# Last layer of a four-layer graph network: the pair product in two row halves of the array

## The chip, the cores and the metric

The kernel runs on one core of a Trainium2 chip. The metric is the device time of one execution in microseconds (us). A core has five engines with instruction queues of their own: PE (TensorE, matrix products; PEld is its loading of weights), DVE (VectorE), ACT (ScalarE), POOL (GpSimd) and SP (SyncE, which here only issues loads). Engines meet only through semaphores.

## The reference

Four graph layers over 4096 nodes with 64 features and a dense 4096x4096 f32 matrix `adj`, each followed by a residual sum and a layer norm. The change lies in the last layer, the hyperbolic one:

```python
def _mobius_add(x, y, c):
    x2 = sum(x * x); y2 = sum(y * y); xy = sum(x * y)
    num = (1.0 + 2.0 * c * xy + c * y2) * x + (1.0 - c * x2) * y
    den = 1.0 + 2.0 * c * xy + c ** 2 * x2 * y2
    return num / maximum(den, MIN_NORM)

sub = _mobius_add(-x_i, x_j, c);  sub_norm = norm(sub)
log_ij = 2.0 / (sqrt_c * lam_x) * arctanh(clip(sqrt_c * sub_norm)) * sub / sub_norm
agg = einsum('ij,ijc->ic', adj / deg, log_ij)
transformed = agg @ weight + bias
x = layernorm(x + expmap(0, transformed))
```

For every pair (i, j) a scalar function of the two points is needed, and then a weighted sum over j of vectors that are linear in x_j. The function depends on one number of the pair, v, which is a product of a vector of i and a vector of j.

## The kernel before, in words

The 4096 nodes are 32 blocks of 128, or 8 groups of 512 (`GB` = 4 blocks a group). Three layers run first; the last one is the block that opens with `with tc.tile_pool(name="o3"`, and its preparation is woven into the end of layer 2.

**Preparation.** `prepare(g)` computes, for the four blocks of a group, the squared norm `n2`, `inside` = 1 - n2, its sign `side`, two flags `sides` (inside or outside the ball), and `rabs` = 1/|inside|. It fills `nat_c` (the rows that the gather sums: x/|inside| in 63 columns, (1 + n2)/|inside| in the last) and `lx`, 66 columns: x, n2 and 1, each times 1/inside. `turn_prepared` transposes `lx` into 66 rows of `tr_a` and `sides` into 2 rows of `tr_o` (bf16, in the memory of `sp_two`), four 128x128 transposes each and one DVE copy each (`to_columns`, L214). `constants3` makes the constants: `to_right`, 66x66, that turns a left vector into a right one, `to_other`, 2x2, for the flags, and `wh_x`, the last weight padded with zeros below row 64.

**The loop.** A tile is a pair of groups (i, j) with j not before i in `seq`: 36 tiles, 8 of them diagonal. Each has two units n of two blocks, so there are NU = 72 units. `right(i)` makes the right operand of a row i: one f32 product of `to_right` with 512 columns of `tr_a`, copied by ACT to `rvs`, and one bf16 product of `to_other`, copied to `ros`. Then, for each unit:

- `product(n)`, L1359, PE: v for two blocks of j against 512 columns of i, two f32 matmuls that contract over 128 rows (66 of them carry data), each into a PSUM bank of its own. There are two `v_ps` buffers, so product(n + 2) waits for the last reader of v of unit n.
- `square(n)`, L1368, ACT: w = (1 + v)^2, the 1 by a bias column.
- `opposite(n)`, L1377, PE: two bf16 matmuls that add 2^60 to v where i and j lie on opposite sides.
- `less_one(n)`, L1385, DVE: w = max(w - 1, floor).
- Ln and Exp on ACT (L1550, L1551) give rt = sqrt(w); DVE adds v to it (L1575, the last reader of v); ACT takes Ln(1 + rt) (L1586) and Exp of w (L1577).
- two units later DVE forms f (L1560) and multiplies the tile of `adj` with it (`at_d`, L1563).
- `turn`, PE L1403: f is transposed, eight 128x128 transposes a unit, for the mirrored tile (j, i), and DVE multiplies (`at_m`, L1405, two a unit). A diagonal tile uses L1396 and L1398 instead.
- `gather`, PE L1419 and L1424: the sums over j for group i in the upper 64 columns of the array and those of the mirrored tile in the lower 64, issued in turns; DVE adds the mirrored sums to `tb` (L1435).

A list `seam` puts one step of other work behind each unit: the end of layer 2 for four groups (`ends`, whose last steps are `prepare` and `turn_prepared`), the `weights` and `factors` of the end, and `finals(g)` for each finished group (L1475 to the store of the output), which multiplies `tr_a` with `wh_x` (L1487).

What sets the order: each engine runs its queue in order. Operations marked `in_order` (the gather here) keep the order of the program among themselves; the rest is placed by the framework's scheduler from its estimates.

Of the kernel before, what the change touches and what calls it, by code (L numbers as in the profile page):

```python
# [9 lines left out]
F32 = mybir.dt.float32  # L10
# [50 lines left out]
def gnn4_kernel(  # L61
# [37 lines left out]
    def gcols(g):  # L99
        return slice(g * GW, (g + 1) * GW)  # L100
# [629 lines left out]

    nat_c = three.tile([P, NB, F], F32, name="nat_c")

    tr_o = sp_two.rearrange("p b f -> p (b f)")
    nat_b = three.tile([P, NB, F], F32, name="nat_b")
    middle = ctx.enter_context(ExitStack())
    late = middle.enter_context(tc.tile_pool(name="late", bufs=1))
# [361 lines left out]
    def prepare(g):  # L1098

        gs = gblocks(g)  # L1100
        xg = nat_a[:, gs, 0:F]
        sq = sm.tile([P, GB, F], F32, name="sq", tag="t0")
        nc.vector.tensor_tensor(sq, xg, xg, ALU.mult)
        nc.vector.tensor_reduce(n2[:, gs], sq, AX.X, ALU.add)
        nc.vector.tensor_scalar(inside[:, gs], n2[:, gs], -1.0, 1.0, ALU.mult, ALU.add)
        nc.vector.tensor_scalar(sides[:, gs, 0], inside[:, gs], 0.0, None, ALU.is_ge)
        nc.vector.tensor_scalar(sides[:, gs, 1], inside[:, gs], 0.0, None, ALU.is_lt)
        nc.vector.tensor_tensor(side[:, gs], sides[:, gs, 0], sides[:, gs, 1], ALU.subtract)
        nc.vector.tensor_tensor(rabs[:, gs], inside[:, gs], side[:, gs], ALU.mult)
        nc.vector.tensor_scalar_max(rabs[:, gs], rabs[:, gs], C_MIN)  # L1110
        nc.vector.reciprocal(rabs[:, gs], rabs[:, gs])
        lx = sm.tile([P, GB, F + 2], F32, name="lx")
        nc.vector.tensor_tensor(lx[:, :, F + 1], rabs[:, gs], side[:, gs], ALU.mult)
        nc.vector.tensor_tensor(lx[:, :, F], n2[:, gs], lx[:, :, F + 1], ALU.mult)
        nc.vector.tensor_tensor(lx[:, :, 0:F], xg, over_rows(lx[:, :, F + 1]), ALU.mult)
        nc.vector.tensor_tensor(nat_c[:, gs, 0 : F - 1], nat_a[:, gs, 0 : F - 1], over_rows(rabs[:, gs], F - 1), ALU.mult)
        nc.vector.scalar_tensor_tensor(nat_c[:, gs, F - 1], n2[:, gs], 1.0, rabs[:, gs], ALU.add, ALU.mult)
        left[g] = lx

    def turn_prepared(ps_p, g):  # L1120
        to_columns(ps_p, tr_a[0 : F + 2, gcols(g)], left.pop(g), F + 2, nc.vector.tensor_copy)
        to_columns(ps_p, tr_o[0:2, gcols(g)], sides[:, gblocks(g), :], 2, nc.vector.tensor_copy)

    def constants3():


        to_right = const.tile([P, F + 2], F32, name="to_right", tag="wih_pp")
        to_other = const.tile([P, 2], BF16, name="to_other", tag="wih_mm")

        spread = const.tile([P, F + 1], F32, name="spread", tag="whh_e")  # L1130
        wh_x = const.tile([P, F], F32, name="wh_x", tag="whh_n")
        nc.vector.memset(to_right, 0.0)
        nc.vector.tensor_scalar_mul(to_right[0:F, 0:F], ident[0:F, 0:F], -4.0)
        nc.vector.tensor_scalar_mul(to_right[F : F + 2, F : F + 1], ident[F : F + 2, F + 1 : F + 2], 2.0)
        nc.vector.tensor_scalar_mul(to_right[F : F + 2, F + 1 : F + 2], ident[F : F + 2, F : F + 1], 2.0)
        nc.vector.memset(to_other, 0.0)
        nc.vector.tensor_scalar_mul(to_other[0:2, 0:1], ident[0:2, 1:2], OPPOSITE)
        nc.vector.tensor_scalar_mul(to_other[0:2, 1:2], ident[0:2, 0:1], OPPOSITE)
        nc.vector.memset(wh_x, 0.0)
        nc.vector.tensor_copy(wh_x[0:F, :], wh)  # L1140
        nc.vector.tensor_copy(spread[:, 0 : F - 1], pair[:, 0 : F - 1])
        nc.vector.tensor_scalar(spread[:, F - 1 : F], pair[:, F - 1 : F], -1.0, None, ALU.add)
        nc.vector.tensor_copy(spread[:, F : F + 1], pair[:, F - 1 : F])
        return to_right, to_other, spread, wh_x
# [146 lines left out]

    with tc.tile_pool(name="o3", bufs=1) as op, tc.tile_pool(name="cols3", bufs=3) as cols_p, tc.tile_pool(
        name="w3", bufs=4
    ) as wp3, tc.tile_pool(name="el3", bufs=3) as el, tc.tile_pool(name="f3", bufs=2) as fp, tc.tile_pool(
# [9 lines left out]

        rvs = [op.tile([P, GW], F32, name=f"rv{q}") for q in range(2)]
        ros = [op.tile([P, GW], BF16, name=f"ro{q}") for q in range(2)]
        for t in rvs + ros:
            nc.gpsimd.memset(t, 0.0)  # L1310

        def right(i):
            q = seq.index(i) % 2
            ps = ps_p.tile([P, GW], F32, name="post", tag="post")
            nc.tensor.matmul(ps[0 : F + 2, :], lhsT=to_right, rhs=tr_a[:, gcols(i)], start=True, stop=True)
            nc.scalar.copy(rvs[q][0 : F + 2, :], ps[0 : F + 2, :])
            ps = ps_p.tile([P, GW], F32, name="post", tag="post")
            nc.tensor.matmul(ps[0:2, :], lhsT=to_other, rhs=tr_o[:, gcols(i)], start=True, stop=True)
            nc.scalar.copy(ros[q][0:2, :], ps[0:2, :])
# [30 lines left out]
        def product(n):  # L1350

            if n >= NU:
                return
            i, j = tiles[n // 2]
            vs[n] = ps_v.tile([P, HB, GW], F32, name="v_ps")
            cs = columns(n)
            for k in range(HB):
                jb = j * CB + (n % 2) * HB + k
                nc.tensor.matmul(  # L1359
                    vs[n][:, k, cs], lhsT=tr_a[:, cols(jb)], rhs=rights[i][0][:, cs], start=True, stop=True  # L1360
                )

        def square(n):
            if n >= NU:
                return
            ws[n] = wp3.tile([P, HB, GW], F32, name="w3")
            cs = columns(n)
            nc.scalar.activation(ws[n][:, :, cs], vs[n][:, :, cs], AF.Square, bias=one_col)  # L1368

        def opposite(n):  # L1370
            if n >= NU:
                return
            i, j = tiles[n // 2]
            cs = columns(n)
            for k in range(HB):
                jb = j * CB + (n % 2) * HB + k
                nc.tensor.matmul(  # L1377
                    vs[n][:, k, cs], lhsT=tr_o[:, cols(jb)], rhs=rights[i][1][:, cs], start=False, stop=True,
                    skip_group_check=True,
                )  # L1380
# [73 lines left out]
        def weights(ps_p):  # L1454
            ps = ps_p.tile([P, GW], F32, name="post", tag="post")
            nc.tensor.transpose(ps[0:F, 0:P], spread[:, 0:F], ident)
            t = sm.tile([F, P], F32, name="spread_t")
            nc.vector.tensor_copy(t, ps[0:F, 0:P])
            ps = ps_p.tile([P, GW], F32, name="post", tag="post")
            nc.tensor.matmul(ps[:, 0:F], lhsT=t, rhs=wh, start=True, stop=True)  # L1460
            nc.vector.tensor_copy(spread_w, ps[:, 0:F])


        def finals(g):
# [73 lines left out]
        while n < NU + 2 or turns or gathers:  # L1538
# [33 lines left out]
            for work in turned:  # L1572
                work()
            if n < NU:
                nc.vector.scalar_tensor_tensor(rt, vs[n][:, :, cs], V_FLOOR, rt, ALU.max, ALU.add)  # L1575
# [64 lines left out]
```

## Time and profile before

Three runs took 1536.35, 1538.62 and 1538.94 us. The profiled execution took 1536.75 us.

| | us |
|---|---|
| median of the runs | 1538.62 |
| profiled execution, whole | 1536.75 |
| its span, first to last instruction | 1535.0 |
| PE busy | 1408.3 (92%) |
| DVE busy | 1064.4 (69%) |
| ACT busy | 762.8 (50%) |
| POOL busy | 124.4 (8%) |
| last layer, first product to end | about 1062 to 1535 |
| its 72 units | 1062 to about 1510 |

The shares over the whole span mix four layers with different limits: in the first, PE and DVE are busy and the matrix is loaded at some 400 GB/s; in the last, DVE, PE and ACT are all near full and the loads are at 110 to 200 GB/s. An f32 matmul stands in the trace as two passes, so two matmuls of a product are four rows. "Idle before" is idle time of the engine in front of an instruction, with what ended it. Where two rows of PE start at the same time, two parts of the array work at once.

### The profile page before, as it was taken

To read this page: it belongs to the slowest core of one execution; us is meant where nothing else is said; L and a number is where in the kernel's file an instruction comes from. 1 tells how busy PE (TensorE), PEld (TensorE's weight loads), DVE (VectorE), ACT (ScalarE), POOL (GpSimd) and SP (SyncE) were. 2 spreads that over 40 slices of the span, in tenths; PEclk is the share of its full clock that TensorE was granted. 3 is DMA by queue.
4 is the path that set the end of the run, shared out by engine and by line. 5 is a ranking of instruction groups with operands and counts; after the bars stand their busy time and mean duration, and the time that the engine had idled before them with its cause. 6 is when DMAs were issued, how large, how long until landed. Compare 5 with 4: busy or idle time off the path is not lost.

```text
span 1535.0 us, 19444 instructions
## 1 busy us (share of the span) xinstructions
PE 1408.3 (92%) x7054; PEld 645.1 (42%) x7054; DVE 1064.4 (69%) x2121; ACT 762.8 (50%) x1267; POOL 124.4 (8%) x194
## 2 busy tenths in 40 slices
PE   5999999999999999889999999998888999899995
PEld 3555555554444333334443333333334434344343
DVE  5889989883000675657677322645999999899997
ACT  3554444432000111212222576655877999899995
POOL 3001100000000011222222200000000000000000
PEclk9999999999999999999999999999999999999997
DMA  9999999996787998878887655453134443445330
GB/s 291 411 406 409 413 409 399 385 357 265 247 278 270 373 387 322 278 280 316 301 317 286 193 170 176 155 165 156 65 141 155 170 168 138 167 160 191 150 114 11
DMA packets 103361, 385.40 MB, mean 251 GB/s; under 512 B 16340, under 2 KB 17368, under 8 KB 71256
## 3 DMA queue, kind: packets, MB, share of 16 engines
q1 hardware_dynamic: 84256, 296.78, 54.1%
q0 software_dynamic: 15616, 85.73, 13.7%
q10 hardware_dynamic: 3384, 1.56, 0.4%
q8 instruction: 58, 0.95, 0.2%
q14 instruction: 47, 0.39, 0.1%
HBM read 297.26 MB, written 85.20 MB: 249 GB/s over the span
## 4 chain that ended last, share of the span: by engine, by line
PE 65%; DVE 20%; ACT 7%; DMA 5%; issue 3%; SPq 0%; ACTq 0%; POOL 0%; DVEq 0%; POOLq 0%
PE tp L604 7%; PE pass L512 6%; PE w_ps L512 6%; PE v_ps L1359 5%; PE sums_ps L1419 4%; PE a_ps L1021 4%; PE cnt_ps L1242 4%; PE acc_ps L1198 4%; PE pass L505 4%; PE h_ps L505 4%; DVE at_m L1405 3%; DVE rt L1575 3%; PE p_ps L1004 2%; PE post L523 2%; ACT wt L1247 2%
## 5 line engine op out<-in xcount | busy, mean ns | idle before, releaser
L611 ACT COPY at<-tp 128x512 f32<-128x512 f32 x256 | 132.5, 599 | 134.6 <-issue 93.7
L1359 PE MATMUL v_ps<-rv,tr_a 128*128 128x512 f32 (+1 forms) x288 | 138.4, 604 | 33.6 <-DVE rt L1575 29.9
L1247 ACT ACTIVATE wt<-cnt_ps 128x512 uint16<-128x512 f32 x210 | 116.4, 594 | 73.8 <-PE cnt_ps L1242 69.6
L604 PE MATMUL tp<-ident,raw 128*128 128x128 f32 x1024 | 133.2, 284 | 14.5 <-DMA raw<-in_adj_dram 9.7
L637 DVE TENSOR_REDUCE dpart<-raw 128x4 f32<-128x2048 f32 x64 | 145.4, 2272 | 0.1
L639 DVE TENSOR_REDUCE lows<-raw 128x1 f32<-128x2048 f32 x64 | 145.4, 2272 | 0.0
L1419 PE MATMUL sums_ps<-at_d,nat_c 128*64 128x512 f32 x288 | 143.2, 619 | 1.4 <-DVE at_d L1563 1.0
L604 PEld LDWEIGHTS tp<-ident,raw 128*128 128x128 f32 x1024 | 116.5, 145 | 53.5 <-issue 30.7
L1021 PE MATMUL a_ps<-at,nat_a 128*64 128x512 f32 x512 | 126.3, 622 | 2.9 <-DVE at L987 2.9
L448 DVE TENSOR_SCALAR pos<-at 128x2048 fp8e4<-128x2048 f32 x72 | 87.6, 1232 | 49.3 <-DMA at<-adj_t 43.3
L1424 PE MATMUL sums_ps<-at_m,nat_c 128*64 128x512 f32 x224 | 111.0, 618 | 0.0
L512 PE MATMUL w_ps<-at,cheb_n 128*128 128x512 f32 x224 | 101.1, 595 | 0.0
L512 PE MATMUL pass<-at,cheb_n 128*128 128x512 f32 x224 | 98.3, 596 | 0.7 <-DVE cheb_n L665 0.7
L1586 ACT ACTIVATE rt<-rt,one_col 128x1024 f32<-128x1024 f32 x72 | 78.7, 1095 | 21.6 <-DVE rt L1575 21.4
L1359 PEld LDWEIGHTS v_ps<-rv,tr_a 128*128 128x128 f32 x288 | 51.9, 195 | 82.8 <-issue 43.4
L1242 PE MATMUL cnt_ps<-m,follow 128*64 128x512 fp8e4 x480 | 81.2, 391 | 5.1 <-ACT wt L1247 2.0
L1575 DVE SCALAR_TENSOR_TENSOR rt<-v_ps,rt 128x1024 f32<-128x1024 f32 x72 | 83.4, 1159 | 3.1 <-ACT rt L1551 2.9
L1560 DVE SCALAR_TENSOR_TENSOR f<-rt,w 128x1024 f32<-128x1024 f32 x72 | 83.0, 1160 | 1.3 <-ACT rt L1586 1.3
L1563 DVE TENSOR_TENSOR at_d<-at_d,f 128x1024 f32<-128x1024 f32 x72 | 83.4, 1159 | 0.1
L1405 DVE TENSOR_TENSOR at_m<-post,at_m 128x512 f32<-128x512 f32 x112 | 75.3, 685 | 10.1 <-PE post L1403 9.5
L1368 ACT ACTIVATE w<-v_ps,one_col 128x1024 f32<-128x1024 f32 x72 | 75.7, 1053 | 11.5 <-PE v_ps L1359 11.0
L1577 ACT ACTIVATE w<-w,half_shift 128x1024 f32<-128x1024 f32 x72 | 78.6, 1094 | 0.8
(368 smaller groups left out, 2269.7 us busy)
## 6 DMA issues: line engine op xcount, KB each, us to landing
at<-adj_t SPq DMA_DIRECT2D x122, 1024.0 KB, 6.6
raw<-in_adj_dram SPq DMA_DIRECT2D x64, 1024.0 KB, 12.3
adj_t<-at POOLq DMA_DIRECT2D x64, 1024.0 KB, 8.1
at_d<-adj_t SPq DMA_DIRECT2D x36, 1024.0 KB, 4.8
at_m<-adj_t SPq DMA_DIRECT2D x28, 1024.0 KB, 6.8
mask_t<-pos POOLq DMA_DIRECT2D x64, 256.0 KB, 6.2
m<-mask_t SPq DMA_DIRECT2D x120, 128.0 KB, 2.8
m<-mask_t SPq DMA_DIRECT2D x60, 256.0 KB, 4.0
```

The lines of the kernel that those rows point to most:

```text
L505: in_order(nc.tensor.matmul(ps[q * F : (q + 1) * F, :], lhsT=cheb_n[:, jb, k, :], rhs=rhs, start=first, stop=last, skip_group_check=True,))
L512: in_order(nc.tensor.matmul(ps, lhsT=cheb_n[:, jb, k : k + 2, :], rhs=rhs, start=first, stop=last))
L604: in_order(nc.tensor.transpose(tp[:, cols(b)], raw[:, b, cols(k)], ident))
L611: nc.scalar.copy(at[:, k, :], tp)
L637: in_order(nc.vector.tensor_reduce(dpart[:, g, c, :], raw, AX.X, ALU.add))
L639: in_order(nc.vector.tensor_reduce(lows[:, n : n + 1], raw.rearrange("p b j -> p (b j)"), AX.X, ALU.min))
L1021: in_order(nc.tensor.matmul(ps[q * F : (q + 1) * F, :], lhsT=nat_a[:, c * CB + k, 0:F], rhs=parts[q if signed else 0][:, k, :], start=(c = ...
L1242: in_order(nc.tensor.matmul(cnt[a][r * HP : (r + 1) * HP, :], lhsT=follow, rhs=chunks[c][odd][2 * a + r][:, k, :], start=(h == 2 * NB - 1) ...
L1247: in_order(nc.scalar.activation(wt[odd][a], cnt[a], AF.Relu, scale=-128.0))
L1359: nc.tensor.matmul(vs[n][:, k, cs], lhsT=tr_a[:, cols(jb)], rhs=rights[i][0][:, cs], start=True, stop=True)
L1419: in_order(nc.tensor.matmul(bank[0:F, :], lhsT=nat_c[:, j * CB + k, :], rhs=own[t][:, k, :], start=(i == j and k == 0), stop=(j == seq[-1] ...
L1575: nc.vector.scalar_tensor_tensor(rt, vs[n][:, :, cs], V_FLOOR, rt, ALU.max, ALU.add)
```

## The change

The pair product is written as 1 + v instead of v, with 64 rows instead of 66, and with the operand of two blocks stacked: block 2m lies in rows 0 to 63 and block 2m + 1 in rows 64 to 127 of the same columns (`tr_c`, half of `tr_a`'s columns). `product` and `opposite` take each block from its half, so two matmuls with 64 rows follow each other in different row halves and write different banks. Both are now marked `in_order`. The left operand becomes `nat_c` times `side`, so that `lx` is one operation. Flags get 64 columns with zeros behind them (`sides`, cleared by POOL for each group), and are transposed two blocks at a time like `lx`. `right` makes each half from a full-height constant that is zero in the other half: four f32 and four bf16 matmuls of 128 columns. As 1 + v is what the product gives, the square and the last Ln lose the bias of 1, and the floor of the DVE step becomes 1 + floor. `finals` uses `tr_c` with a `wh_x` per half, which is made from `spread_w`. The clearing of `tr_o`, `rvs` and `ros` on POOL goes.

```diff
+    tr_c = tr_a[:, 0 : N // 2].rearrange("p (m n) -> p m n", n=P)
+    tr_o = sp_two[:, 0 : NB // 2, :]
...
-    nc.gpsimd.memset(tr_o, 0.0)
...
+        sides = sm.tile([P, GB, F], F32, name="sides", tag="o_sb")
+        nc.gpsimd.memset(sides, 0.0)
...
-        lx = sm.tile([P, GB, F + 2], F32, name="lx")
-        nc.vector.tensor_tensor(lx[:, :, F + 1], rabs[:, gs], side[:, gs], ALU.mult)
-        nc.vector.tensor_tensor(lx[:, :, F], n2[:, gs], lx[:, :, F + 1], ALU.mult)
-        nc.vector.tensor_tensor(lx[:, :, 0:F], xg, over_rows(lx[:, :, F + 1]), ALU.mult)
...
+        lx = sm.tile([P, GB, F], F32, name="lx")
+        nc.vector.tensor_tensor(lx, nat_c[:, gs, :], over_rows(side[:, gs]), ALU.mult)
...
     def turn_prepared(ps_p, g):
-        to_columns(ps_p, tr_a[0 : F + 2, gcols(g)], left.pop(g), F + 2, nc.vector.tensor_copy)
-        to_columns(ps_p, tr_o[0:2, gcols(g)], sides[:, gblocks(g), :], 2, nc.vector.tensor_copy)
+        ps = ps_p.tile([P, 2 * GB // 2, P], F32, name="post", tag="post")
+        ms = slice(g * GB // 2, (g + 1) * GB // 2)
+        for n, t in enumerate(left.pop(g)):
+            for m in range(GB // 2):
+                two = t[:, 2 * m : 2 * m + 2, :].rearrange("p b f -> p (b f)")
+                nc.tensor.transpose(ps[:, n * GB // 2 + m, :], two, ident)
+        nc.vector.tensor_copy(tr_c[:, ms, :], ps[:, 0 : GB // 2, :])
+        nc.vector.tensor_copy(tr_o[:, ms, :], ps[:, GB // 2 : GB, :])
...
+        to_right = const.tile([P, 2, P], F32, name="to_right", tag="whh_n")
+        to_other = const.tile([P, 2, P], BF16, name="to_other", tag="wih_mm")
+        wh_x = const.tile([P, 2, F], F32, name="wh_x", tag="wih_pp")
...
+        for q in range(2):
+            half = slice(q * F, (q + 1) * F)
+            two = slice(q * F, q * F + 2)
+            for c in range(2):
+                nc.vector.tensor_copy(to_right[half, q, c * F : (c + 1) * F], w[half, :])
...
         def right(i):
...
+            for to, w, t in ((rvs[q], to_right, tr_c), (ros[q], to_other, tr_o)):
+                ps = ps_p.tile([P, GW], F32, name="post", tag="post")
+                for b in range(GB):
+                    nc.tensor.matmul(
+                        ps[:, cols(b)], lhsT=w[:, b % 2, :], rhs=t[:, (i * GB + b) // 2, :], start=True, stop=True
+                    )
+                nc.scalar.copy(to, ps)
...
-                nc.tensor.matmul(
-                    vs[n][:, k, cs], lhsT=tr_a[:, cols(jb)], rhs=rights[i][0][:, cs], start=True, stop=True
-                )
+                half = slice(jb % 2 * F, jb % 2 * F + F)
+                in_order(nc.tensor.matmul(
+                    vs[n][:, k, cs], lhsT=tr_c[half, jb // 2, :], rhs=rights[i][0][half, cs], start=True, stop=True
+                ))
...
-            nc.scalar.activation(ws[n][:, :, cs], vs[n][:, :, cs], AF.Square, bias=one_col)
+            nc.scalar.activation(ws[n][:, :, cs], vs[n][:, :, cs], AF.Square)
...
-                    vs[n][:, k, cs], lhsT=tr_o[:, cols(jb)], rhs=rights[i][1][:, cs], start=False, stop=True,
-                    skip_group_check=True,
+                half = slice(jb % 2 * F, jb % 2 * F + F)
+                in_order(nc.tensor.matmul(
+                    vs[n][:, k, cs], lhsT=tr_o[half, jb // 2, :], rhs=rights[i][1][half, cs],
+                    start=False, stop=True, skip_group_check=True,
+                ))
...
+            for q in range(2):
+                half = slice(q * F, (q + 1) * F)
+                nc.vector.tensor_copy(wh_x[half, q, :], spread_w[half, :])
...
-                nc.vector.scalar_tensor_tensor(rt, vs[n][:, :, cs], V_FLOOR, rt, ALU.max, ALU.add)
+                nc.vector.scalar_tensor_tensor(rt, vs[n][:, :, cs], 1.0 + V_FLOOR, rt, ALU.max, ALU.add)
...
-                nc.scalar.activation(rt, rt, AF.Ln, bias=one_col)
+                nc.scalar.activation(rt, rt, AF.Ln)
```

More of the change, by code (lines that the diff above doesn't have):

```diff
@@ L731, in gnn4_kernel @@
     nat_c = three.tile([P, NB, F], F32, name="nat_c")
-    tr_o = sp_two.rearrange("p b f -> p (b f)")
+    tr_c = tr_a[:, 0 : N // 2].rearrange("p (m n) -> p m n", n=P)
+    tr_o = sp_two[:, 0 : NB // 2, :]
     nat_b = three.tile([P, NB, F], F32, name="nat_b")
@@ L1088, in gnn4_kernel @@
     front.close()
-    nc.gpsimd.memset(tr_o, 0.0)
     inside = const.tile([P, NB], F32, name="inside")
-    sides = const.tile([P, NB, 2], F32, name="sides")
     side = const.tile([P, NB], F32, name="side")
@@ L1105, in prepare @@
         nc.vector.tensor_scalar(inside[:, gs], n2[:, gs], -1.0, 1.0, ALU.mult, ALU.add)
-        nc.vector.tensor_scalar(sides[:, gs, 0], inside[:, gs], 0.0, None, ALU.is_ge)
-        nc.vector.tensor_scalar(sides[:, gs, 1], inside[:, gs], 0.0, None, ALU.is_lt)
-        nc.vector.tensor_tensor(side[:, gs], sides[:, gs, 0], sides[:, gs, 1], ALU.subtract)
+        nc.vector.tensor_scalar(sides[:, :, 0], inside[:, gs], 0.0, None, ALU.is_ge)
+        nc.vector.tensor_scalar(sides[:, :, 1], inside[:, gs], 0.0, None, ALU.is_lt)
+        nc.vector.tensor_tensor(side[:, gs], sides[:, :, 0], sides[:, :, 1], ALU.subtract)
         nc.vector.tensor_tensor(rabs[:, gs], inside[:, gs], side[:, gs], ALU.mult)
@@ L1111, in prepare @@
         nc.vector.reciprocal(rabs[:, gs], rabs[:, gs])
-        lx = sm.tile([P, GB, F + 2], F32, name="lx")
-        nc.vector.tensor_tensor(lx[:, :, F + 1], rabs[:, gs], side[:, gs], ALU.mult)
-        nc.vector.tensor_tensor(lx[:, :, F], n2[:, gs], lx[:, :, F + 1], ALU.mult)
-        nc.vector.tensor_tensor(lx[:, :, 0:F], xg, over_rows(lx[:, :, F + 1]), ALU.mult)
         nc.vector.tensor_tensor(nat_c[:, gs, 0 : F - 1], nat_a[:, gs, 0 : F - 1], over_rows(rabs[:, gs], F - 1), ALU.mult)
         nc.vector.scalar_tensor_tensor(nat_c[:, gs, F - 1], n2[:, gs], 1.0, rabs[:, gs], ALU.add, ALU.mult)
-        left[g] = lx
+        lx = sm.tile([P, GB, F], F32, name="lx")
@@ L1120, in turn_prepared @@
+        nc.vector.tensor_tensor(lx, nat_c[:, gs, :], over_rows(side[:, gs]), ALU.mult)
+        left[g] = lx, sides
     def turn_prepared(ps_p, g):
-        to_columns(ps_p, tr_a[0 : F + 2, gcols(g)], left.pop(g), F + 2, nc.vector.tensor_copy)
-        to_columns(ps_p, tr_o[0:2, gcols(g)], sides[:, gblocks(g), :], 2, nc.vector.tensor_copy)
+        ps = ps_p.tile([P, 2 * GB // 2, P], F32, name="post", tag="post")
[4 more added lines that the diff above has]
+                nc.tensor.transpose(ps[:, n * GB // 2 + m, :], two, ident)
@@ L1124, in constants3 @@
+        nc.vector.tensor_copy(tr_c[:, ms, :], ps[:, 0 : GB // 2, :])
+        nc.vector.tensor_copy(tr_o[:, ms, :], ps[:, GB // 2 : GB, :])
     def constants3():
-        to_right = const.tile([P, F + 2], F32, name="to_right", tag="wih_pp")
-        to_other = const.tile([P, 2], BF16, name="to_other", tag="wih_mm")
+        to_right = const.tile([P, 2, P], F32, name="to_right", tag="whh_n")
+        to_other = const.tile([P, 2, P], BF16, name="to_other", tag="wih_mm")
         spread = const.tile([P, F + 1], F32, name="spread", tag="whh_e")
-        wh_x = const.tile([P, F], F32, name="wh_x", tag="whh_n")
+        wh_x = const.tile([P, 2, F], F32, name="wh_x", tag="wih_pp")
@@ L1132, in constants3 @@
+        w = sm.tile([P, F], F32, name="w_right", tag="scrap")
+        not_last = sm.tile([P, 1], F32, name="not_last", tag="low")
+        nc.vector.tensor_scalar(not_last, pair[:, F - 1 : F], -1.0, 1.0, ALU.mult, ALU.add)
+        nc.vector.tensor_scalar(w[:, 0 : F - 1], pair[:, 0 : F - 1], 1.0, -4.0, ALU.add, ALU.mult)
+        nc.vector.tensor_scalar(w[:, 0 : F - 1], w[:, 0 : F - 1], not_last, None, ALU.mult)
+        nc.vector.tensor_copy(w[:, F - 1 : F], pair[:, F - 1 : F])
         nc.vector.memset(to_right, 0.0)
-        nc.vector.tensor_scalar_mul(to_right[0:F, 0:F], ident[0:F, 0:F], -4.0)
@@ L1134, in constants3 @@
-        nc.vector.tensor_scalar_mul(to_right[F : F + 2, F : F + 1], ident[F : F + 2, F + 1 : F + 2], 2.0)
-        nc.vector.tensor_scalar_mul(to_right[F : F + 2, F + 1 : F + 2], ident[F : F + 2, F : F + 1], 2.0)
         nc.vector.memset(to_other, 0.0)
-        nc.vector.tensor_scalar_mul(to_other[0:2, 0:1], ident[0:2, 1:2], OPPOSITE)
-        nc.vector.tensor_scalar_mul(to_other[0:2, 1:2], ident[0:2, 0:1], OPPOSITE)
         nc.vector.memset(wh_x, 0.0)
-        nc.vector.tensor_copy(wh_x[0:F, :], wh)
+        for q in range(2):
[3 more added lines that the diff above has]
+                nc.vector.tensor_copy(to_right[half, q, c * F : (c + 1) * F], w[half, :])
+                for n in range(2):
+                    k = q * F + 1 - n
+                    nc.vector.tensor_scalar_mul(
+                        to_other[two, q, c * F + n : c * F + n + 1], ident[two, k : k + 1], OPPOSITE
+                    )
@@ L1308, in gnn4_kernel @@
         ros = [op.tile([P, GW], BF16, name=f"ro{q}") for q in range(2)]
-        for t in rvs + ros:
-            nc.gpsimd.memset(t, 0.0)
         def right(i):
             q = seq.index(i) % 2
[L1314 to L1319, printed above, removed]
+            for to, w, t in ((rvs[q], to_right, tr_c), (ros[q], to_other, tr_o)):
[3 more added lines that the diff above has]
+                        ps[:, cols(b)], lhsT=w[:, b % 2, :], rhs=t[:, (i * GB + b) // 2, :], start=True, stop=True
+                    )
+                nc.scalar.copy(to, ps)
             return rvs[q], ros[q]
@@ L1376, in opposite @@
                 jb = j * CB + (n % 2) * HB + k
-                nc.tensor.matmul(
-                    vs[n][:, k, cs], lhsT=tr_o[:, cols(jb)], rhs=rights[i][1][:, cs], start=False, stop=True,
-                    skip_group_check=True,
-                )
+                half = slice(jb % 2 * F, jb % 2 * F + F)
[3 more added lines that the diff above has]
+                ))
         def less_one(n):
@@ L1486, in second @@
                     nc.tensor.matmul(o[:, b, 0, :], lhsT=tb[:, cols(jb)], rhs=spread_w, start=True, stop=True)
-                    nc.tensor.matmul(o[:, b, 1, :], lhsT=tr_a[:, cols(jb)], rhs=wh_x, start=True, stop=True)
+                    nc.tensor.matmul(o[:, b, 1, :], lhsT=tr_c[:, jb // 2, :], rhs=wh_x[:, jb % 2, :], start=True, stop=True)
                 t = sm.tile([P, GB, F], F32, name="agg", tag="t0")
```

## The prediction

> **What bounds the kernel now.** I read the busy slices first (the last third is where VectorE, DVE, is at 9 tenths in nearly every slice), then the last layer by stages, its groups, the waits of DVE, and the timelines of a steady stretch. The change touches nothing that runs before about 1058 us except small set-up work, so only the stage from 1060 us on is summed. Busy time by stage; after the length come PE, PEld, DVE, ACT, POOL, and then the granted clock:
>
> ```profile
> core 0: us, PE busy (x) PEld busy (x) DVE busy (x) ACT busy (x) POOL busy (x), PEclk, DMA share, GB/s
> 1060.00:1120.00 60.00, 49.22 (x178) 22.42 (x177) 52.14 (x135) 47.29 (x56) 1.38 (x3) 0.91 0.41 159
> 1120.00:1280.00 160.00, 142.96 (x599) 62.02 (x600) 155.75 (x258) 140.58 (x159) 0.00 (x0) 0.99 0.42 159
> 1280.00:1440.00 160.00, 145.93 (x592) 63.21 (x591) 147.95 (x238) 144.97 (x201) 0.00 (x0) 0.98 0.42 157
> 1440.00:1510.00 70.00, 64.35 (x283) 30.03 (x283) 65.97 (x121) 62.04 (x104) 0.00 (x0) 1.00 0.31 114
> ```
>
> From 1060 to 1510 us DVE is busy 52.14 + 155.75 + 147.95 + 65.97 = 421.8 of 450 us; only 28.2 us are idle. PE has 402.5, ACT 394.9. DVE is the bound, PE and ACT follow closely. The last 25 us, with DVE at 15.3, are a chain of short steps and stay. What ended DVE's idle time between 1060 and 1510 us:
>
> ```profile
> DVE at_m L1405 <- PE post L1403: 9.5, 10, 2.2
> DVE w L1385 <- ACT w L1368: 4.8, 2, 4.0
> DVE tb L1435 <- PE sums_ps L1424: 3.6, 4, 2.4
> DVE rt L1575 <- ACT rt L1551: 2.9, 4, 1.5
> DVE tr_a L214 <- PE post L213: 1.3, 1, 1.3
> ```
>
> PE stands behind 9.5 + 3.6 + 1.3 and two waits of 0.4 and 0.2, 15.0 us, and behind the 4.8 through the square that reads its product: 19.8 us. ACT alone has 5.6 (2.9 and smaller ones), 2.8 are short gaps. That is what a faster PE can reach, though it will have far more than that to give.
>
> **The product and the opposite sides.** One unit of the steady stretch: the product's four passes (two blocks, two passes each), the gather's passes in column halves, the opposite matmuls.
>
> ```profile
> 1257.54 1.98 PE L1359 MATMUL v_ps<-rv,tr_a 128*128 128x512 f32 x4 [0.47 <-DVE rt L1575]
> 1259.45 0.64 PE L1419 MATMUL sums_ps<-at_d,nat_c 128*64 128x512 f32 x1
> 1259.46 0.64 PE L1424 MATMUL sums_ps<-at_m,nat_c 128*64 128x512 f32 x1
> 1259.93 0.59 PE L1419 MATMUL sums_ps<-at_d,nat_c 128*64 128x512 f32 x1
> ...
> 1260.36 0.59 PE L1419 MATMUL sums_ps<-at_d,nat_c 128*64 128x512 f32 x1
> ...
> 1261.33 0.60 PE L1377 MATMUL v_ps<-ro,sp_two 128*128 128x512 bf16 x2
> ```
>
> A pass of 512 columns takes 0.43 us (1259.93 to 1260.36). Each pass of L1419 starts with one of L1424: two halves of the array work at once, and eight passes take 1.88 us. The product's four take 1.91 (1257.54 to 1259.45), one after another. No f32 matmul in row halves stands in this trace. Bounds: paired like the column halves, 1.91 - 2 x 0.43 = 1.05 us; not paired, 1.91. In layer 2, bf16 matmuls of 64 rows do start in pairs:
>
> ```profile
> 1052.25 0.39 PE L1198 MATMUL acc_ps<-wt,over_two 64*128 64x512 bf16 x1
> 1052.26 0.39 PE L1198 MATMUL acc_ps<-wt,sup_two 64*128 64x512 bf16 x1
> 1052.48 0.38 PE L1198 MATMUL acc_ps<-wt,over_two 64*128 64x512 bf16 x1
> ```
>
> Both neighbours (f32 in column halves, 64 rows in bf16) pair, so I take 1.05: 0.86 us saved in each of the 64 full units and 0.43 in the 8 half-wide ones, 58.5 us of PE. The opposite pair drops from two slots of 0.22 (1052.26 to 1052.48) to one: 64 x 0.22 + 8 x 0.11 = 15.0 us. PE now changes between whole array and column halves twice a unit; with row halves four times. Such a change can cost between nothing and the 0.19 by which 1.91 exceeds 4 x 0.43; I take half, 2 x 72 x 0.10 = 14 us. PE is relieved by 58.5 + 15.0 - 14 = 59 us.
>
> The Trainium skill speaks against the change here: "TensorEngine Tiling (Array Packing)", Key Properties, says that a change of tiling mode drains the engine. With the whole 0.19 for each of 144 further changes that would be 27 us instead of 14, and PE would still gain 46.
>
> **What of it reaches the end.** DVE's part of a unit, by starts:
>
> ```profile
> 1251.07 1.22 DVE L1575 SCALAR_TENSOR_TENSOR rt<-v_ps,rt 128x1024 f32<-128x1024 f32 x1
> 1252.20 0.69 DVE L1385 TENSOR_SCALAR w<-w 128x1024 f32<-128x1024 f32 x1
> 1252.80 1.22 DVE L1560 SCALAR_TENSOR_TENSOR f<-rt,w 128x1024 f32<-128x1024 f32 x1
> ```
>
> Three of 1.13 (L1575, L1560, L1563), one of 0.60 (L1385), two at_m of 0.60 (L1405) and half a tb of 0.7: 5.55 us. PE: 1.91 + 1.88 + 0.44 + 1.04 (eight transposes, L1403) = 5.27. PE's margin is 0.28 us before and 5.55 - (5.27 - 0.86 - 0.22 + 0.20) = 1.16 after. So of 59 us most only turns into idle PE. What counts is PE being late: 15.0 us in some 17 waits, the longest 2.4. With 0.9 us more margin a unit PE makes up 1.8 us in two units; short waits vanish, the two above 2 us shrink. Bounds: none of the 15.0 goes, or all. I take two thirds, 10. At the start of the layer DVE waits 4.0 us for right, product and square; the product comes 0.86 earlier, and in the changed issue order y (L1168 before, 0.75 for two) stands ahead of w, so 2 us of it go (0.9 to 4.0).
>
> **DVE's own work.** For each of the four groups prepared in this stage, two small lx (0.16 each) and one of 0.42 become one of 0.42, and two copies out of PSUM of 512 columns (0.68, 0.67) become two of 256 columns (0.42 each, by L1492 of that size): 0.83 less, 3.3 in all. wh_x gets two copies of 64x64 (0.16 to 0.42 each; 0.2 taken): 2.9 us less. These lie in a stretch where DVE is full (1120 to 1160 us), so they count.
>
> **Costed at nothing.** On POOL, the clearing of tr_o (3.5 us at 850 us) goes, where the next POOL work starts at 916; those of rv and ro (1.5 us from 1058.95) go, done before ACT's copies need them or within 0.1 us. The new clears of sides run on a POOL that has nothing else; if DVE met one late, some 0.3 us a group. to_right, to_other and w_right: some 25 small DVE operations, in the first layers and in layer 2, where DVE is at 2 to 6 tenths of a slice; uncovered, 25 x 0.16 = 4 us. right makes eight f32 passes of 128 columns and four bf16 instead of two and one of 512: at 0.13 a pass (L1403, 1.04 for eight) 1.04 + 0.3 against 1.07 + 0.22, the same; ACT's two copies are as wide as before. Square and Ln lose their bias operand: same width, nothing. SP's loads keep their order.
>
> **The clock.** After an idle stretch PE is slow:
>
> ```profile
> 1313.68 3.78 PE L1359 MATMUL v_ps<-rv,tr_a 128*128 128x512 f32 x4 [2.21 <-DVE rt L1575]
> ```
>
> 1.8 us longer than at 1257.54, the gather behind it 1.2: PE comes 3.0 us late and DVE then waits 2.4 and 2.2. An idle PE is what this change makes. I allow three more such stretches; between 0.7 (3.0 less two margins) and 3.0 each on DVE, mostly absorbed: 2.5 us in all (0 to 9).
>
> "TensorE: Matmul & The Clock Gate", Part 1, puts the fall to half clock behind a whole idle window of some 3.4 us; here 2.2 us of waiting, after one of 0.5, was enough. By the page no gap of a unit would bring it, and the sum would be 14.9; by this row it is 12.4.
>
> **Sum.** 10 + 2 + 2.9 = 14.9, less 2.5: 12.4 us. The profiled execution took 1536.75, its span 1535.0: span 1522.6, execution 1524.4. The median of the runs is 1.87 above that execution, so the forecast is 1526.2.
>
> **Rivals.**
> - All waits on PE go, and some of ACT's too (PE's margin quadruples; against it, ACT has 394.9 of 450 us and will set small waits): 15 + 4 + 2.9 + 3 of ACT's, 1514.
> - The gain is hidden: DVE is 94% busy, the waits come back as waits on ACT. Only DVE's own 2.9 remain: 1535.7. For it: 21 us in which ACT waits for DVE at L1586, two engines passing delays to each other.
> - f32 row halves don't pair, so the change doesn't do what it says. PE pays 14 us of changes, which use up 0.20 of the 0.28 us a unit: some 5 us late, less 2.9: 1541. Both paired neighbours speak against.
> - Slower: the clock. PE's busy share falls from 89% to 76% of the 450 us; if one unit in three (24) starts at half clock, at 1.5 us each, 36 us go against 14.9 won: 1560. It decides from some ten such stretches on. Against it: PE at 31 of 40 us, from 1120 to 1160, kept 0.99.
>
> **How the numbers follow.** Forecast 57%, all waits 15%, hidden 14%, not paired 6%, clock 8%. The range 1511 to 1538 holds the forecast, most of the second case (28.3 us, all waits whatever their cause and DVE's 2.9, would give 1510) and the third; the last two are outside. A time within 0.2% (3.1 us) can't be told from no change. Faster: 57 + 15 and a third of hidden, 0.77; same: the rest of hidden and a bit of not paired, 0.11; slower 0.12.
>
> **What would show it.** The product's four passes at two starts, 1.05 us to the gather; PE some 345 us busy from 1060 on instead of 402; DVE's idle time there near 15, its waits on at_m and tb below 6 us; DVE busy about 3 us less. The prediction is wrong if passes start singly, if the granted clock falls below 0.95 in a stage after 1120, or if DVE's idle time stays near 28 with ACT named behind it.

## The result, and the profile after

The changed kernel takes 1528.65 us (median of 5 runs, 1525.96 to 1530.22) beside 1537.65 us for the kernel before in the same session (5 runs, 1536.35 to 1538.94): a ratio of 0.9946, 95% interval 0.9928 to 0.9965. It is 9.0 us faster. The forecast of 1526.2 us had the sign and the range right, and the pairing works as it said; the gain it summed, 12.4 us, was too large, and its main term came out much smaller than forecast. The profiled execution took 1529.61 us with a span of 1527.9, 7.1 less than the span before.

The same stages of the last layer, with the columns as before (length, PE, PEld, DVE, ACT, POOL, granted clock, DMA share, GB/s). The last unit now ends near 1503 instead of 1510:

```profile
core 0: us, PE busy (x) PEld busy (x) DVE busy (x) ACT busy (x) POOL busy (x), PEclk, DMA share, GB/s
1060.00:1120.00 60.00, 45.70 (x181) 18.66 (x182) 52.27 (x133) 48.27 (x59) 0.62 (x2) 0.83 0.43 168
1120.00:1280.00 160.00, 126.87 (x591) 52.23 (x591) 152.00 (x250) 133.05 (x155) 0.00 (x0) 0.91 0.41 154
1280.00:1440.00 160.00, 137.64 (x662) 59.18 (x658) 152.97 (x253) 145.64 (x208) 0.00 (x0) 0.96 0.45 166
1440.00:1503.00 63.00, 52.07 (x266) 24.25 (x266) 61.37 (x111) 55.53 (x97) 0.00 (x0) 1.00 0.29 105
```

From 1060 to 1503 DVE is busy 418.6 of 443 us, so it idles 24.4 (28.2 before) and does 3.2 less work (421.8 before). The two make up the 7.0 by which this stage is shorter, of the span's 7.1: nearly the whole difference lies in this layer (layer 2 ends 0.17 earlier). PE is busy 362.3 us instead of 402.5, and its clock in the second row is 0.91 where it was 0.99. One steady unit on PE in the timeline (start, length, engine and line, tiles, shape, count, idle time before it and what ended that):

```profile
1242.77 1.13 PE L1381 MATMUL v_ps<-rv,tr_a 64*128 64x512 f32 x4 [0.47 <-DVE rt L1601]
1243.83 0.64 PE L1442 MATMUL sums_ps<-at_d,nat_c 128*64 128x512 f32 x1
1243.84 0.64 PE L1447 MATMUL sums_ps<-at_m,nat_c 128*64 128x512 f32 x1
...
1245.72 0.39 PE L1400 MATMUL v_ps<-ro,sp_two 64*128 64x512 bf16 x2
```

Four f32 passes of 64 rows take 1.06 us to the gather (1242.77 to 1243.83), where the four passes of 128 rows took 1.91. The product's own wait for DVE's rt, 0.47 us, is the one that it had before. That PE is further ahead shows in its other waits, from 1060 to 1510 before (us in total, times, longest):

```profile
PE post L1403 <- DVE at_m L1405: 5.5, 11, 1.1
PE v_ps L1377 <- ACT w L1368: 0.8, 3, 0.3
```

and from 1060 to 1503 now:

```profile
PE v_ps L1400 <- ACT w L1390: 14.7, 28, 2.0
PE post L1426 <- DVE at_m L1428: 13.3, 21, 1.1
```

In all, PE has 40.2 us less to do and idles 33.2 us more (80.7 instead of 47.5). What ended DVE's idle time between 1060 and 1505:

```profile
DVE tb L1456 <- PE sums_ps L1447: 5.5, 3, 2.3
DVE at_m L1428 <- PE post L1426: 4.7, 6, 1.9
DVE rt L1601 <- ACT rt L1577: 2.8, 4, 0.9
DVE y L1189 <- PE post L1183: 2.7, 1, 2.7
DVE f L1586 <- ACT rt L1612: 2.0, 3, 0.9
DVE tb L1458 <- PE sums_ps L1447: 1.2, 1, 1.2
```

at_m fell from 9.5 to 4.7 and w, which waited 4.8 through the square, to 0.3. But tb rose from 4.0 to 6.7, and y, which waited 0.2, now waits 2.7 at the start of the layer. The two longest tb waits, 2.00 and 2.29, lie where a group is prepared. All engines there, in the timeline:

```profile
1153.29 1.02 PE L1381 MATMUL v_ps<-rv,tr_a 64*128 64x512 f32 x4
...
1159.30 0.66 PE L1128 MATMUL post<-ident,lx 128*128 128x128 f32 x2 [4.99 <-DVE lx L1118]
...
1160.32 1.12 PE L1442 MATMUL sums_ps<-at_d,nat_c 128*64 128x512 f32 x1
...
1161.22 1.06 PE L1442 MATMUL sums_ps<-at_d,nat_c 128*64 128x512 f32 x1
...
1164.07 0.69 DVE L1456 COPY tb<-sums_ps 64x512 f32<-64x512 f32 x1 [2.29 <-PE sums_ps L1447]
```

PE has finished the product by 1154.3, and then the transposes of lx stand at the head of its queue and wait 4.99 us for DVE's preparation (2.86 at the same place before). The gather behind them then runs at half speed, 0.90 from pass to pass instead of 0.43, and DVE waits 2.29 for its sums. The kernel before had a smaller loss of the same kind here:

```profile
1158.14 0.60 PE L213 MATMUL post<-ident,lx 128*66 128x128 f32 x4 [2.86 <-DVE nat_c L1117]
1163.31 1.29 DVE L1405 TENSOR_TENSOR at_m<-post,at_m 128x512 f32<-128x512 f32 x2 [1.80 <-PE post L1403]
```

From 1160 to 1165 its granted clock was 0.71; in the changed kernel it is 0.53. At the preparation ahead of this one, near 1144, it had no such loss: the clock stayed at 1.00 and DVE did not wait, where it now waits the 2.00.

### The profile page after: what moved, and what is told of

Its sections match the earlier page's. It is cut to its first block, busy times and chain, and to the rows that moved or that the text cites. A ratio compares the mean times of both kernels' runs of the same rounds, so it can differ in the third digit from the quotient of the medians.

```text
span 1527.9 us, 19545 instructions
## 1 busy us (share of the span) xinstructions
PE 1362.6 (89%) x7094; PEld 618.2 (40%) x7094; DVE 1060.1 (69%) x2117; ACT 750.1 (49%) x1267; POOL 122.7 (8%) x197
## 4 chain that ended last, share of the span: by engine, by line
PE 51%; DVE 25%; ACT 9%; DMA 7%; issue 6%; ACTq 1%; POOL 0%; SPq 0%; DVEq 0%; POOLq 0%
PE pass L512 7%; PE w_ps L512 6%; PE tp L604 6%; PE cnt_ps L1263 4%; PE acc_ps L1219 4%; PE pass L505 4%; DMA raw<-in_adj_dram 3%; DVE at_m L1428 3%; DVE rt L1601 3%; PE a_ps L1024 3%; DVE f L1586 3%; PE h_ps L505 3%; DVE at_d L1589 3%; PE sums_ps L1442 2%; PE post L523 2%
## 5 line engine op out<-in xcount | busy, mean ns | idle before, releaser
L1442 PE MATMUL sums_ps<-at_d,nat_c 128*64 128x512 f32 x288 | 152.9, 656 | 2.2 <-DVE at_d L1589 1.0
L1024 PE MATMUL a_ps<-at,nat_a 128*64 128x512 f32 x512 | 122.5, 605 | 2.9 <-DVE at L990 2.9
L1447 PE MATMUL sums_ps<-at_m,nat_c 128*64 128x512 f32 x224 | 118.9, 657 | 0.0
L1381 PE MATMUL v_ps<-rv,tr_a 64*128 64x512 f32 (+1 forms) x288 | 86.3, 679 | 33.9 <-DVE rt L1601 33.7
L1612 ACT ACTIVATE rt<-rt 128x1024 f32<-128x1024 f32 x72 | 72.2, 1006 | 26.8 <-DVE rt L1601 26.6
L1426 PE MATMUL post<-ident,f 128*128 128x128 f32 x448 | 70.4, 286 | 14.9 <-DVE at_m L1428 13.3
L1577 ACT ACTIVATE rt<-w,half_shift 128x1024 f32<-128x1024 f32 x72 | 79.2, 1100 | 0.7
```

The costliest lines, as they stand in the source:

```text
L1024: in_order(nc.tensor.matmul(ps[q * F : (q + 1) * F, :], lhsT=nat_a[:, c * CB + k, 0:F], rhs=parts[q if signed else 0][:, k, :], start=(c = ...
L1442: in_order(nc.tensor.matmul(bank[0:F, :], lhsT=nat_c[:, j * CB + k, :], rhs=own[t][:, k, :], start=(i == j and k == 0), stop=(j == seq[-1] ...
```

## The experiments

The first group asks what carries the gain.

**Both matmuls of a unit in the same row half.** Blocks are stacked in another order, so that the two blocks of a unit lie in one half; the instructions are those of the changed kernel, but for lx in two operations for each group.

```diff
-                half = slice(jb % 2 * F, jb % 2 * F + F)
+                half = slice(jb // 2 % 2 * F, jb // 2 % 2 * F + F)
-                    vs[n][:, k, cs], lhsT=tr_c[half, jb // 2, :], ...
+                    vs[n][:, k, cs], lhsT=tr_c[half, jb // 4 * 2 + jb % 2, :], ...
```

> The changed kernel with the blocks stacked in another order: block b of a group lies in row half b // 2 and not b % 2, so the two matmuls of a unit use the same row half, with the same instructions on every engine otherwise (lx is two operations of 128 columns on DVE in place of one of 256). Theory (the pairing alone makes the gain): the product's four passes start one after another, 1.91 us, PE near 400 us from 1060 us on, time 1532 to 1538. Rival (the zero-padded variant lost its time through ACT's further copies and the later start, the pairing is worth little): 1527 to 1531.

Its timeline:

```profile
1242.19 1.98 PE L1387 MATMUL v_ps<-rv,tr_a 64*128 64x512 f32 x4 [0.36 <-DVE rt L1607]
1244.10 0.64 PE L1448 MATMUL sums_ps<-at_d,nat_c 128*64 128x512 f32 x1
```

The same 64-row passes take 1.91 us (1242.19 to 1244.10) when they share a half. 1539.36 us, ratio to the kernel before 1.0038 [1.0017, 1.0058]. That is just above the 1532 to 1538 expected. Without the pairing all the rest of the change is a loss of some 6 us; by this run the pairing is worth about 14 us (1.0038 less 0.9946, 0.0092 of the time).

**One of the two put in the same half.** The edit above, for the opposite matmuls alone and for the product alone.

> The product keeps its two row halves; the two opposite matmuls of a unit are put into the same half, so they run one after another (0.44-0.53 us instead of 0.22); all else as in the changed kernel. Theory (the gain comes from PE time given back, and most of PE's margin lies hidden behind DVE): about 0.25 us of a unit's margin goes, the kernel stays within 3 us of the changed one, 1528 to 1532. Rival (every bit of PE time counts, as the loss with both in one half, 10 us for 1.1 us a unit, would say in proportion): 2.5 us slower, no difference that can be told. Rival (the mode changes around the opposite matmuls are what costs): no gain over the kernel before, 1536 to 1539.

> The opposite matmuls keep their two row halves; the two product matmuls of a unit are put into the same half (1.91 us instead of 1.06); lx is written by two operations of 128 columns instead of one of 256 for each group (some 0.1 us each on DVE, four groups). Theory: the product carries the gain, so this is no faster than the kernel before: 1536 to 1540, product at 1.9 us, PE busy about 400 in the last layer. Rival (the lighter DVE and ACT work and the earlier start carry half of it): 1531 to 1534.

Opposite unpaired: 1528.14 us, 0.9932 [0.9905, 0.9959], not to be told from the changed kernel, though the pair takes 0.21 us longer to the transposes behind it (0.53 instead of 0.32). Product unpaired: 1547.43 us, 1.0072 [1.0046, 1.0099], slower still than the 1536 to 1540 expected. Its timeline:

```profile
1249.90 0.39 PE L1405 MATMUL v_ps<-ro,sp_two 64*128 64x512 bf16 x2
1251.89 1.98 PE L1386 MATMUL v_ps<-rv,tr_a 64*128 64x512 f32 x4 [0.47 <-DVE rt L1606]
```

Here the opposite pair stays in one slot and the product is back at its old length. So the product's pairing is the gain, and the opposite sides' pairing brings nothing that can be measured. Why this kernel is slower than the one with neither paired (the intervals just overlap) was not settled; its clock from 1120 to 1280 was 0.90, there 0.95, and DVE's waits for tb come to 13.0 us, there 7.1.

**No row halves, but 1 + v.** The right operand gets a zero half, so that the matmuls have 128 rows again (POOL clears it, and ACT copies by halves).

```diff
-                    vs[n][:, k, cs], lhsT=tr_c[half, jb // 2, :], rhs=rights[i][0][half, cs], ...
+                    vs[n][:, k, cs], lhsT=tr_c[:, jb // 2, :], rhs=rights[i][0][jb % 2][:, cs], ...
```

> The changed kernel with the row halves taken away: product and opposite contract over all 128 rows, and the right operand of each block has zeros in the other half, so the same numbers come out of the same layout, one matmul after another. ACT makes four half copies instead of two full ones for each of the 8 rows of groups (some 1.2 us a row). Theory (the pairing gives the gain of PE, DVE's smaller preparation the rest): four passes of the product take 1.91 us again, PE is near 400 us busy from 1060 us on, the time is 1533 to 1539. Rival (the pairing is idle, the lighter preparation and the new issue order give the gain): 1527 to 1531, as the changed kernel.

1537.03 us, 1.0011 [0.9994, 1.0029]: no gain without the pair, and by this run the pairing is worth some 10 us (1.0011 less 0.9946) and not 14. It is the weaker proof, since its clears delay the first product by about 2 us and ACT has more copies.

**The bias back.** Square and Ln get a column of zeros as bias.

```diff
-            nc.scalar.activation(ws[n][:, :, cs], vs[n][:, :, cs], AF.Square)
+            nc.scalar.activation(ws[n][:, :, cs], vs[n][:, :, cs], AF.Square, bias=zero_col)
...
-                nc.scalar.activation(rt, rt, AF.Ln)
+                nc.scalar.activation(rt, rt, AF.Ln, bias=zero_col)
```

> The square and the logarithm of the last layer get a bias operand back, a column of zeros (one POOL clear of it at the layer's start); the numbers are the same. Theory (ACT is not the bound; PE's relief is the gain): the square takes 1.10 us instead of 1.01 and the logarithm 1.14 instead of 1.05, ACT is 13 us busier over the layer, and the time stays within 2 us of the changed kernel, 1527 to 1531. Rival (ACT's lighter operations, which the prediction put at nothing, are a part of the gain): 3 to 8 us slower than the changed kernel, 1532 to 1537, with DVE waiting longer on ACT's rt.

Groups of the changed kernel, 1120 to 1500 us (busy, mean ns, idle before):

```profile
L1612 ACT ACTIVATE rt<-rt 128x1024 f32<-128x1024 f32 x56 | 58.8, 1055 | 18.7 <-DVE rt L1601 18.4
L1390 ACT ACTIVATE w<-v_ps 128x1024 f32<-128x1024 f32 x54 | 54.5, 1009 | 3.4 <-PE v_ps L1381 3.2
```

The same groups with the bias:

```profile
L1614 ACT ACTIVATE rt<-rt,zero_col 128x1024 f32<-128x1024 f32 x56 | 64.0, 1143 | 12.0 <-DVE rt L1603 11.6
L1392 ACT ACTIVATE w<-v_ps,zero_col 128x1024 f32<-128x1024 f32 x55 | 60.5, 1100 | 4.2 <-PE v_ps L1383 4.2
```

The operand costs 88 to 91 ns an operation, 11 us of ACT's time over the layer. The kernel takes 1526.4 us, 0.9933 [0.991, 0.9957]: nothing of it reaches the end. ACT only waits less for DVE (11.6 instead of 18.4).

**Order.** `in_order` is taken away from product and opposite.

```diff
-                in_order(nc.tensor.matmul(vs[n][:, k, cs], ...))
+                nc.tensor.matmul(vs[n][:, k, cs], ...)
```

> The changed kernel without the fixed program order of product and opposite, so that the scheduler places them as it did before. Theory (order matters little, DVE and the clock set the time): within 3 us of the changed kernel. Rival (the fixed order makes PE wait in front of opposite for ACT's square, 14.7 us in 28 waits, and this holds the transposes and the gather back): 4 to 8 us faster, and those waits fall below 5 us.

1527.53 us, 0.9942 [0.992, 0.9963]: the same as the changed kernel, and PE still waits 12.1 us for ACT's w. The fixed order neither makes nor costs the gain.

The second group asks how much room PE has.

**Opposite matmuls issued twice in the kernel before** (+0.44 us a unit, 32 us of PE), **and four times in the changed one** (+0.66 a unit, 47 us). The repetitions add the same term again, so the sums of v are others.

```diff
-            for k in range(HB):
+            for k in [k for _ in range(2) for k in range(HB)]:
```

> The kernel before with the opposite matmuls issued twice: 0.44 us more PE work a unit, 32 us in all, against a margin that I put at 0.28 us a unit. Theory (PE was close behind DVE before): slower than before by 8 to 25 us, 1545 to 1562, well more than 47 us of added PE work costs the changed kernel. Rival (PE had hidden margin before too, the gain comes from elsewhere): within 4 us of before.

> The changed kernel with the opposite matmuls issued four times in place of once (the big number is added four times; the pair function is clipped there either way), 0.66 us more PE work a unit, 47 us in all, with no new wait for another engine. Theory of the clock (half clock after idle stretches costs part of the gain): the granted clock in the last layer rises to 0.97 or more and the time falls by 2 to 8 us, to 1520 to 1527. Rival (PE has margin, the clock's loss is hidden as well): the clock rises, the time stays within 3 us of 1528.6. If PE were still the bound it would grow by more than 20 us.

Before, doubled: 1539.87 us, 1.0031 [1.0011, 1.005]: 4.7 us for 32 us of work, less than the 8 to 25 expected and close to the rival's 4. Changed, four times: 1554.53 us, 1.0126 [1.0098, 1.0155], far beyond either expectation, and no clean test: PE is busy only 384.7 of 468 us and its clock stays at 0.91 in the second stage. What PE waits for in it:

```profile
PE v_ps L1400 <- ACT w L1390: 34.8, 26, 2.6
PE sums_ps L1442 <- DVE at_d L1421: 14.4, 6, 2.8
```

In its timeline the order of a unit has changed: transposes, then the opposite passes, then the product, so PE stands at the opposite passes until ACT has squared, the product comes late, and DVE waits 17.0 us for rt. What it measures is this loop of waits between in-order queues, not the price of PE time.

**Half of at_d's product on POOL.** Is DVE alone the bound?

```diff
-                nc.vector.tensor_tensor(at, at, f, ALU.mult)
+                nc.vector.tensor_tensor(at[:, 0:1], at[:, 0:1], f[:, 0:1], ALU.mult)
+                nc.gpsimd.tensor_tensor(at[:, 1:2], at[:, 1:2], f[:, 1:2], ALU.mult)
```

> The changed kernel with DVE's product of the tile and the factor (1.13 us a unit) shared: one of the two blocks goes to POOL, which is idle here. DVE has 0.53 us a unit less, 38 us in all. Theory (DVE is the bound after the change, ACT next with 5.2 us a unit): 10 to 25 us faster than the changed kernel, 1504 to 1518. Rival (POOL takes so long for 512 elements, or slows DVE's own work, that the gather waits): 1530 to 1580, with the gather waiting for POOL or DVE's mean durations above 1.25 us.

Its groups, 1120 to 1500 us:

```profile
L1590 POOL TENSOR_TENSOR at_d<-at_d,f 128x512 f32<-128x512 f32 x55 | 83.1, 1515 | 268.2 <-DVE f L1586 82.5 <-PE v_ps L1381 71.5 <-issue 20.8
L1589 DVE TENSOR_TENSOR at_d<-at_d,f 128x512 f32<-128x512 f32 x56 | 59.3, 1059 | 0.0
```

1537.35 us, 1.0019 [1.0001, 1.0037], some 11 us above the changed kernel (0.0073) where a gain of 10 to 25 had been expected. DVE's half takes 1059 ns where 128x512 takes 683 alone and the whole took 1215: with POOL at work beside it, halving the operation saves DVE 0.16 us. So this did not lighten DVE and can't answer the question.

The third group asks where the rest of the forecast gain is: is it the clock, or the queue at the group preparations?

**PE kept busy.** Four matmuls with zero weights into the open sums bank before each product; then eight at units with a step of the seam and two otherwise.

```diff
+                idle_work(4)
                 product(n + 2)
```

> The changed kernel with four further bf16 matmuls of 512 columns with zero weights ahead of each product, which add zeros to the open sums: 0.88 us of PE a unit, inside its margin of 1.16. Theory (an idle PE falls to half clock, and what is late after it costs a good part of the gain): the granted clock in the last layer rises from 0.91 to 0.98 or more, DVE's idle time falls from 24 to below 18, and the time is 3 to 8 us shorter, 1521 to 1526. Rival (the clock is harmless, the rest is latency between ACT and DVE): the clock rises and the time stays or grows by up to 5 us, since PE has less margin.

> The same added matmuls, eight in a unit that has a step of other work behind it, where DVE is full and PE waits longest, and two in the others. Theory: the slow stretches lie where DVE has the further work, so this does at least as well as four everywhere: 1519 to 1525. Rival (clock harmless): no gain, 1528 to 1535.

With four, the stages and DVE's waits:

```profile
1120.00:1280.00 160.00, 140.69 (x679) 59.14 (x677) 152.10 (x250) 134.66 (x157) 0.00 (x0) 0.96 0.41 153
1280.00:1440.00 160.00, 148.00 (x749) 64.95 (x746) 150.90 (x249) 144.77 (x208) 0.00 (x0) 1.00 0.45 165
```

```profile
DVE w L1408 <- ACT w L1390: 6.6, 8, 2.0
DVE at_m L1428 <- PE post L1426: 5.2, 7, 1.8
```

The clock rises from 0.91 and 0.96 to 0.96 and 1.00 and tb's waits fall to 1.2, yet DVE idles 24.2 us as in the changed kernel, since w now waits 6.6 for a product that stands behind the fillers. 1531.55 us, 0.9965 [0.9944, 0.9986]. The larger filling gives 1551.26 us, 1.010 [1.0073, 1.0127], far above what theory and rival expected. The fillers also write the gather's bank and so add waits of their own; they don't show what a faster clock alone would bring.

**The seam's step behind the gather.** The same instructions, with preparations, transposes and final steps issued after a unit's gather.

```diff
             after = gather(*gathers.pop(n)) if n in gathers else []
+            if n and seam:
+                seam.pop(0)(ps_p)
...
-            if seam:
-                seam.pop(0)(ps_p)
```

> The changed kernel with the last layer's step of the seam (group ends, preparation and its transposes, the final steps) issued after the gather of a unit instead of before it; the same instructions, another place. In the changed kernel's trace the transposes of lx stand ahead of a gather whose operands are long there, wait 2.17 and 4.99 us for DVE's lx, and DVE then waits 2.00 and 2.29 us for the sums (tb). Theory (these two waits are gain of the change given back at the group preparations, because the gather is stuck behind the transposes): they go, DVE's waits on tb fall from 6.7 us to 3 or less, and the time is 3 to 5 us below the changed kernel, 1523 to 1526. Rival (the waits only move: PE then waits for lx behind the gather, in front of the transposes of f, and at_m is late instead): at_m rises by what tb loses, and the time stays within 2 us of the changed kernel, 1527 to 1530.

DVE's waits from 1060 to 1507 us:

```profile
DVE sq L1503 <- PE post L1501: 5.2, 3, 2.3
DVE at_m L1428 <- PE post L1426: 4.2, 9, 0.9
DVE w L1408 <- ACT w L1390: 3.7, 5, 0.8
...
DVE tb L1458 <- PE sums_ps L1447: 1.1, 2, 0.7
```

tb falls from 6.7 to 1.1, as the theory said: the gather was stuck behind the transposes. But the final steps were moved too, and sq now waits 5.2 for their matmuls, w 3.7. 1535.21 us, 1.0002 [0.9977, 1.0026]: outside both expectations, and the whole gain over the kernel before is gone. The rival is right that the waits move, though not to at_m and not at equal cost, as it had it. Moving the preparation's transposes alone was not tried.

## Why the prediction was right, and where its size was off

- **Rows pair.** Forecast 1.05 us for the product, measured 1.06; opposite forecast at one slot of 0.22, measured 0.23 where the product follows (1153.06 to 1153.29) and 0.32 where the transposes follow. In the same half the product's passes take 1.91. The further changes between whole array and halves, put at 0.10 us each, cost the product next to nothing: it now exceeds 2 x 0.43 by 0.20, where it had exceeded 4 x 0.43 by 0.19. The pairing is shown, and the product's pairing is shown to be the gain.
- **DVE is the bound, PE's relief mostly turns into idle PE.** That neither ACT's nor PE's load is the bound is shown from three sides: ACT 11 us heavier costs nothing that can be measured, nor does 0.21 us more PE a unit with the opposite unpaired, and the 32 us added before cost 4.7. That DVE's load is the bound rests on its busy share, 418.6 of 443 us; no run made DVE lighter, so it isn't shown by experiment. The estimate of PE's margin before, 0.28 us a unit, was too small for this: 0.44 a unit is 0.16 beyond it, and 0.16 x 72 = 11.5.
- **DVE's own work.** Forecast 2.9 less, measured 3.2. Only two of the four preparations lie in the stretch from 1120 to 1160 that the prediction named; the others are near 1092 and 1104.
- **Start of the layer.** Forecast 2, measured 1.2: the wait of 3.97 for w is gone, one of 2.74 for y stands ahead of it.
- **The steady waits are the mis-sized term.** Of 15.0 us ended by PE the forecast took 10 away and gave 2.5 back to the clock, 7.5 net. In the profile at_m, tb, tr_a, the later w and small ones (before: 9.5 + 4.0 + 1.3 + 0.8 + 0.2 = 15.8; after: 4.7 + 6.7 + 0.7 + 0.3 + 0.3 + 0.2 = 12.9) fell by 2.9. Waits ended by ACT stayed: 5.6 and 5.9. 3.2 + 1.2 + 2.9 - 0.3 = 7.0, the difference found above; the medians differ by 9.0. The step that failed is therefore this net term, forecast 7.5 and measured 2.9. Two of the named signs missed with it: DVE's idle time is 24.4, not near 15, and its waits on at_m and tb come to 11.4. That the total still came within 2.4 us of the forecast owes something to chance.
- **What stood in that term's place.** Stretches of slow clock, and the queue in front of them. In slices of 5 us from 1120 on, the changed kernel has ten stretches with a granted clock below 0.9, the kernel before two; the forecast had allowed three more. Four of the ten have a DVE wait for PE right behind them, and these are all the tb waits: 2.29 and 2.00 at the group preparations, where the transposes of lx stand in front of a ready gather, and twice 1.19, near 1200 and 1281. With 0.20 for at_m that is 6.9 us; the two stretches before had 6.4 (1.80, 2.41 and 2.16). The prediction had the long waits shrink; they did not. The other waits from 1120 on, for PE and for the square that reads its product, did fall as forecast, from 6.9 to 2.0; those between the layer's start and 1120, where the clock was 0.83 instead of 0.91, rose from 2.5 to 3.6.
- **The clock in particular.** The prediction had taken 1120 to 1160 as safe, because PE at 31 of 40 us kept 0.99 there. That reading ended just too early: the kernel before fell to 0.71 in the 5 us that follow. With PE at 25.9 of the same 40 us the clock is now 0.80, and 0.50 in the worst 5 us. A granted clock below 0.95 after 1120 was named as a sign of a wrong prediction, and the 0.91 came. PE's busy time is 362 and not 345 because slow passes count longer: the gather's 504 passes of 512 columns alone took 267.9 us instead of 250.3. That slow clock and queue together cost the missing 5 us is the likeliest reading, but it isn't shown that the time can be had: two experiments each removed the tb waits and neither gained.
- **Rivals.** "Hidden" and "not paired" are excluded by the interval and by the passes' starts. "All waits go" failed, as PE still ends 15 us of DVE's idle time. "Slower: the clock" had its condition met, about ten slow stretches, and still failed: six of the ten have no DVE wait for PE right behind them.

## What to carry to other kernels

Two 64-row matmuls into different banks and different row halves run at once, in f32 as in bf16; it is worth doing where that engine's lateness, not its load, is in the bound engine's waits, and the gain is read from those waits, not from the time saved on PE. Before summing the gain, look at what stands at the head of the freed engine's in-order queue: time that it gains in front of an instruction waiting for the bound engine is lost, and the idle stretch can lower its clock for the work behind. A short operation that rides on the large one (here the opposite sides) need not be paired too.

## What the runs showed of the hardware

Half clock came after shorter waits than expected. In the changed kernel's timeline:

```profile
1276.79 1.60 PE L1381 MATMUL v_ps<-rv,tr_a 64*128 64x512 f32 x4 [1.57 <-DVE rt L1601]
1278.32 1.11 PE L1442 MATMUL sums_ps<-at_d,nat_c 128*64 128x512 f32 x1
...
1279.22 1.06 PE L1442 MATMUL sums_ps<-at_d,nat_c 128*64 128x512 f32 x1
```

After 1.57 us of waiting the product took 1.53 us and the gather 0.90 a pass, twice its usual 0.43; full speed was back by 1280.84. The granted clock was 1.00 in each 2 us from 1268 to 1276, 0.83 in the next and 0.50 from 1278 to 1280. Taken finer it was 1.00 up to 1277.2 and 0.50 from 1277.4: it fell when PE was at work again. The Trainium skill, "TensorE: Matmul & The Clock Gate", Part 1, names an idle window of about 3.4 us as what brings half clock; here a wait of less than half of that was enough, with shorter gaps of 0.22 to 0.51 in the 15 us ahead of it, and the measurement decides. Nor does the length of a single wait settle it: in the kernel before, a product that had waited 3.74 us (1140.92) took its usual time, and the granted clock stayed at 1.00. What decides was not tested.

Leaving out a bias operand shortens a 128x1024 ACT operation by 88 to 91 ns, which the prediction had put at nothing. The Trainium skill, "ScalarE: Activation LUTs", section "What ACT_TABLE_LOAD costs", gives about 93 ns for each such per-partition operand, and these rows agree with it.
